# Starting each front one pair earlier, ScalarE on both halves of the features, and the linear attention term once per pair

## The chip, the core and the metric

The kernel runs on one core of a Trainium2 chip. The metric is the time of the device for one execution, in microseconds (us). The engines of the core work side by side, each through its own instructions in the order in which the program put them: TensorE (PE in the profile; PEld is its load of weights) multiplies matrices, VectorE (DVE), ScalarE (ACT) and GpSimd (POOL) work on elements, SyncE (SP) issues transfers. An engine that has to wait for another holds up all that stands behind the waiting instruction.

## The reference

The input x has 64 graphs of 256 nodes with 128 features, in float32, and all share one 256 x 256 matrix adj. Four layers follow each other, each of the form x = x + layer(relu(layernorm(x))). Cut to what matters (e is short for the 256 hidden features of the last layer):

```python
# layer 0: five steps of a gated graph network
m  = adj @ h;  u = h @ u3.T
z, r = sigmoid([m, m] @ w3.T + u), sigmoid([m, m] @ w4.T + u)
hv = tanh([m, m] @ w5.T + (r * h) @ u5.T)
h  = (1 - z) * h + z * hv
# layer 1: h, adj.T h, 2 adj.T adj.T h - h (each twice), one matrix, relu
# layer 2: ((adj + 1) h) @ weight + bias, each row over its norm
# layer 3: attention over all pairs of nodes i, j
pre = s1[:, :, None, :] + s2[:, None, :, :] + b_lin      # 256 x 256 x 256 for each graph
e   = einsum('bije,e->bij', leaky_relu(pre, 0.2), a) + adj
out = sigmoid(softmax(e, axis=2) @ x)
```

Layer 3 is the bulk: for each graph 65536 pairs of nodes with 256 hidden features each, which are clipped and then summed over the features with the weights a. s1 and s2 are x times the two halves of a 256 x 256 matrix W, and in this model W is adj itself.

## The kernel before

**Pairs of graphs.** The 64 graphs are worked on in 32 pairs (`NB = 2`). Most tiles are 128 partitions by 2 x 256 float32, with features on the partitions.

**The front of a pair** (`front`, a Python generator) is all that comes before the attention: layers 0 to 2, the norm of layer 3, its transpose hT, and the operands of the attention. These are s2a (s2 of the first 128 hidden features, with the sign turned; it stays in one of two PSUM banks), s2n (the same for the second 128, copied to SBUF), s1a and s1b (s1 plus b_lin for each half, by ScalarE). It is one long chain: nearly every step needs the one before, on another engine. Three PSUM banks (`spare`) are shared by the fronts in progress and the tails.

**Tiles of the attention.** The leaky relu is split as 0.2 pre + 0.8 relu(pre). For the second part, a "tile" (`rl`, 128 hidden features x 4 nodes i x 2 graphs x 256 nodes j) holds, for four nodes i, either min(s1, -s2) or relu(s2 + s1): both serve, with weights of opposite signs, since they differ by a term that is the same for all j and so drops out of the softmax. A pair has 64 slots for each half of the features, 128 tiles in all:
- VectorE makes every tile of the first half (half 0): one minimum of 2048 elements, line 628, from s1a and the PSUM bank s2a.
- ScalarE and GpSimd share the tiles of the second half (half 1). ScalarE takes eight activations of 256 elements a tile (line 641), from a copy of s2n in PSUM (`s2p`, line 635), GpSimd eight minima of 256 elements (line 647), from s2n in SBUF. An engine makes the next slot of half 1 whenever it is free.
Thirteen buffers `rl` are shared. At most 8, 3 and 2 of them are held by VectorE, ScalarE and GpSimd (`MOST`).

**Scoring.** TensorE multiplies each tile by a window of the weights a (four matmuls of 32 columns each, line 685 in `score`) and sums 64 tiles into one PSUM bank. So a pair has two blocks of 128 nodes i (`ic`), and two banks `pes` take turns. The first thing summed into each block is the linear term 0.2 a W2 h (`project(pe, g2, hT)` in `score`); its part that depends only on i drops out of the softmax.

**The tail of a block** (`tail`): VectorE adds adj to the scores (sc, line 543, which frees the bank), takes the maximum (nmx, line 547), ScalarE the exponential, TensorE transposes and multiplies by h3, ScalarE takes the tanh, GpSimd finishes, SyncE stores.

**What sets the order.** A scheduler in Python, at the end of the kernel, runs while the program is written. It holds a clock for each engine, adds a cost for each group of instructions (`ran`) and, at each step, gives the engine that is furthest behind the most urgent of what is ready by that reckoning: steps of a tail first, then steps of a front, then tiles or scoring. The result is a fixed order of instructions on each engine. `SEEN` is the time until another engine can use a result. Where the order is wrong for the chip, the engines wait for each other's semaphores.

**When fronts run.** Two fronts begin at the start; after that, these lines decide when the next one begins and how fast it may go:

```python
        while begun_fronts[0] < NPAIR and begun_fronts[0] < 2 + scored[0] // (2 * SLOTS):
            begin_front()
...
            due = STEPS_OF_FRONT * (scored[0] / (2 * SLOTS) - (key - 2)) / SPREAD
            if CHAINS[key][2] > due + AHEAD:
                return None
```

A pair has `2 * SLOTS` = 128 tiles, so front p + 2 begins when all tiles of pair p have been scored, which is about when pair p + 1 starts. `due` is how many of a front's 106 steps may have been taken; with `SPREAD` 1.8 and `AHEAD` 8, some 67 of them may be taken at once at that point. A tile of a pair can be made only when its front is done: `READY[p]` holds the operands, and `since` the times at which each half can start.

Of the kernel before, what the change touches and what calls it, by code (L numbers as in the profile page):

```python
# [8 lines left out]
F32 = mybir.dt.float32  # L9
AF = mybir.ActivationFunctionType  # L10
# [5 lines left out]
NB = 2  # L16
# [9 lines left out]
def kernel(  # L26
# [65 lines left out]


    clock = dict.fromkeys((PE, DVE, ACT, POOL), 0.0)
    SEEN = {PE: 0.25, DVE: 0.14, ACT: 0.45, POOL: 0.13}

    def ran(engine, us, *after):
        clock[engine] = max(clock[engine], 0.0, *after) + us
        return clock[engine] + SEEN[engine]

    spare = [[b, 0.0] for b in banks[5:]]

# [34 lines left out]
    def load_x(p):  # L137
        if p >= NPAIR:
            return
        XIN[p] = work.tile([P, NB, NC, D], F32, name="xin", bufs=3)  # L140
        for b in range(NB):
            nc.sync.dma_start(XIN[p][:, b], x[p * NB + b].rearrange("(c p) d -> p c d", p=P))

# [29 lines left out]
    def load_transposed(w, name, scale=None):  # L173

        cols = w.shape[1]
        raw = work.tile([P, 2 * D], F32, name="w_raw", bufs=3)
        nc.scalar.dma_start(raw[:, :cols], w)
        src = raw[:, :D]
        if cols == 2 * D:
            s = work.tile([P, D], F32, name="w_sum")  # L180
            nc.vector.tensor_add(s, raw[:, :D], raw[:, D:])
            src = s
        pt = bank([P, P], "pt")
        nc.tensor.transpose(pt, src, ident)
        t = const.tile([P, P], F32, name=name)
        if scale is None:
            nc.vector.tensor_copy(t, pt)
        else:
            nc.vector.tensor_scalar(t, pt, scale, None, op0=OP.mult)
        return t  # L190
# [44 lines left out]
    nc.vector.memset(win_n, 0.0)  # L235
    w2n = const.tile([P, N], F32, name="w2n")
    nc.vector.tensor_scalar(w2n, adj_t[:, 1, :], -1.0, None, op0=OP.mult)
    a_rep = const.tile([P, NE, P], F32, name="a_rep")
    nc.vector.memset(a_rep, 1.0)
    for k in range(NE):  # L240
        nc.vector.tensor_scalar(win[:, k, 31:32], acol[:, k:k + 1], 1.0 - ALPHA, None, op0=OP.mult)
# [62 lines left out]
    def rows_of(t):  # L304
        return t.rearrange("p b c d -> p (b c) d")

    SHORT = dict(tag="short", bufs=14)


    PROJECT, MIX, TURN, PRODUCT, PRODUCTS = 0.86, 1.74, 0.69, 0.88, 2.64  # L310
# [28 lines left out]
        spare.append([bank[0], t])  # L339
        return c, t  # L340

    KEPT = {"hT": dict(bufs=4), "hT3": {}, "s2n": {}}

    READY = {}

    def front(p):
# [163 lines left out]
        yield PE, max(t_hT, t_s2v[p % 2])  # L510
        project(s2a, w2n[:, 0:P], hT)
        t_s2a = ran(PE, PROJECT, t_hT, t_s2v[p % 2])
        yield PE, t_hT, 1
        b = take()
        project(b[0], w2n[:, P:2 * P], hT)
# [18 lines left out]
        nc.scalar.activation(s1a, by_feature(b[0]), AF.Identity, bias=blin[:, 0:1], scale=1.0)  # L534
        t_n = ran(ACT, BIASED, t)
        spare.append([b[0], t_n])
        READY[p] = dict(x3=x3, h3=h3, hT=hT, s1=(s1a, s1b), s2a=by_feature(s2a), s2n=s2n, since=(max(t_n, t_s2a), max(t_b, t_2)))

    def tail(p, ic, pe, since, x3, h3):

        yield DVE, since
        sc = feat("sc", **SHORT)
        nc.vector.tensor_add(sc, by_feature(pe), adj_n[:, ic, :].unsqueeze(1).to_broadcast([P, NB, N]))
        t_pe[p * NC + ic] = ran(DVE, ELEMENTS, since)
        yield DVE, clock[DVE]
        nmx = work.tile([P, NB], F32, name="nmx")
        nc.vector.tensor_reduce(nmx, sc, AX.X, OP.max, negate=True)
        t = ran(DVE, ELEMENTS)
        yield ACT, t
        sums = work.tile([P, NB], F32, name="sums")  # L550
        for b in range(NB):
            nc.scalar.activation(sc[:, b, :], sc[:, b, :], AF.Exp, bias=nmx[:, b:b + 1], scale=1.0,  # L552
                                 accum_out=sums[:, b:b + 1])
        t_s = ran(ACT, 1.0, t)
        yield PE, t_s, 1
        b = take()
        to_token(b[0], sc)
        t = ran(PE, TURN, t_s, b[1])
        yield ACT, t
        wT = tok("wT", **SHORT)  # L560
        nc.scalar.mul(wT, by_token(b[0]), 0.5)
        t = ran(ACT, COPY, t)
        spare.append([b[0], t])
        yield PE, t, 1
        b = take()
        po = b[0][:, :NB * D].rearrange("p (b d) -> p b d", b=NB)
        for k in range(NB):
            for c in range(NC):
                side_by_side(po[:, k, :], wT[:, k, c, :], h3[:, k, c, :], c == 0, c == NC - 1)
        t = ran(PE, PRODUCT, t, b[1])  # L570
        yield DVE, t_s
        rs = work.tile([P, NB], F32, name="rs")
        nc.vector.reciprocal(rs, sums)
        t_s = ran(DVE, 0.08, t_s)
        yield ACT, max(t, t_s)
        o = work.tile([P, NB, D], F32, name="o")
        for k in range(NB):
            nc.scalar.activation(o[:, k, :], po[:, k, :], AF.Tanh, scale=rs[:, k:k + 1])
        t = ran(ACT, 0.5, t, t_s)
        spare.append([b[0], t])  # L580
        yield POOL, t
        nc.gpsimd.tensor_scalar(o, o, 0.5, 0.5, op0=OP.mult, op1=OP.add)
        nc.gpsimd.tensor_add(o, o, x3[:, :, ic, :])
        ran(POOL, 1.1, t)
        nc.sync.dma_start(out[p * NB:(p + 1) * NB, ic * P:(ic + 1) * P, :].rearrange("b p d -> p b d"), o)
        TAILED.add((p, ic))
# [8 lines left out]
    made = []  # L595
    left = {}
    t_pe = {}
    t_s2v = [0.0, 0.0]
    TAILED = set()

    def where(n):
        return n // SLOTS, n % SLOTS // 32, n % 32

    def tile_ready(e):

        if e in begun:
            return 0.0
        n = following[e != DVE]
        if n >= NSLOT or n // SLOTS not in READY or held[e] == MOST[e] or not tiles:
            return None  # L610
        return max(READY[n // SLOTS]["since"][e != DVE], min(t[1] for t in tiles))

    def work_on_tile(e):
        k = int(e != DVE)
        if e not in begun:
            tiles.sort(key=lambda t: t[1])
            begun[e] = [following[k], *tiles.pop(0), 0]
            following[k] += 1
            held[e] += 1
        n, t, free, part = begun[e]  # L620
        p, ic, r = where(n)
        ops = READY[p]
        i0 = ic * P + r
        since = max(ops["since"][k], free)
        if e == DVE:
            whole = [P, 4, NB, N]
            rows = ops["s1"][0][:, :, i0:i0 + 97:32].rearrange("p b g -> p g b").unsqueeze(3)
            nc.vector.tensor_tensor(t, rows.to_broadcast(whole), ops["s2a"].unsqueeze(1).to_broadcast(whole), op=OP.min)  # L628
            done = ran(DVE, 2.2, since)
            t_s2v[p % 2] = done  # L630
            parts = 1
        elif e == ACT:
            if "s2p" not in ops:
                ops["s2p"] = s2p
                nc.scalar.copy(s2p, ops["s2n"])
                ran(ACT, COPY, since)
            parts = 2
            for g in (2 * part, 2 * part + 1):
                for b in range(NB):
                    i = i0 + g * 32  # L640
                    nc.scalar.activation(t[:, g, b, :], s2p[:, b, :], AF.Relu, bias=ops["s1"][1][:, b, i:i + 1], scale=-1.0)  # L641
            done = ran(ACT, 1.43, since)
        else:
            parts = 4
            for b in range(NB):
                i = i0 + part * 32
                nc.gpsimd.tensor_scalar(t[:, part, b, :], ops["s2n"][:, b, :], ops["s1"][1][:, b, i:i + 1], None, op0=OP.min)  # L647
            done = ran(POOL, 1.8, since)
        begun[e][3] += 1
        if part + 1 == parts:  # L650
            del begun[e]
            made.append((done, n, k, t, e))
# [18 lines left out]
    def score(tile_):  # L671
        since, n, k, t, e = tile_
        p, ic, r = where(n)
        block = p * NC + ic
        pe = pes[block % 2]
        if block not in left:
            left[block] = 64
            project(pe, g2, READY[p]["hT"], stop=False)
            ran(PE, PROJECT, t_pe.get(block - 2, 0.0))
        made.remove(tile_)  # L680
        left[block] -= 1

        w = win if e == ACT else win_n
        for g in range(4):
            nc.tensor.matmul(pe[g * 32:(g + 1) * 32, :], w[:, k, 31 - r:63 - r], flat(t[:, g]),  # L685
                             start=False, stop=(left[block] == 0), skip_group_check=True)
        free = ran(PE, PROJECT, since)
        tiles.append([t, free])
        held[e] -= 1
        scored[0] += 1  # L690
        if left[block] == 0:
            begin((p, ic), tail(p, ic, pe, free, READY[p]["x3"], READY[p]["h3"]))


    CHAINS = {}
    STEPS_OF_FRONT, SPREAD, AHEAD = 106, 1.8, 8
    begun_fronts = [0]

    def begin(key, steps):
# [8 lines left out]
    def chain_ready(key, e):  # L708

        engine, since, bank, gate = (*CHAINS[key][1], 0, None)[:4] if len(CHAINS[key][1]) < 4 else CHAINS[key][1]  # L710
        if engine != e or bank and not spare or gate and not gate():
            return None
        if not isinstance(key, tuple) and key > 0:

            due = STEPS_OF_FRONT * (scored[0] / (2 * SLOTS) - (key - 2)) / SPREAD
            if CHAINS[key][2] > due + AHEAD:
# [12 lines left out]
    for e in clock:  # L729
        clock[e] = 0.0  # L730
    while scored[0] < 2 * NSLOT or CHAINS:
        while begun_fronts[0] < NPAIR and begun_fronts[0] < 2 + scored[0] // (2 * SLOTS):
            begin_front()
        e = min(now, key=now.get)
        todo = []
# [57 lines left out]
```

## Time and profile before

| | before |
|---|---|
| median of 3 runs | 5523.23 us (5520.46 to 5524.22) |
| span of the profiled execution | 5520.6 us |
| mean granted TensorE clock | 0.997 |
| busy: PE, DVE, ACT, POOL | 5376.7, 5314.8, 5012.2, 5038.5 us |
| HBM traffic | 3 GB/s over the span |
| last step of the first front (s1a) | at 145.4 us |
| first pair on DVE | 145.4 to 298.4 us, the second to 469.1 us |
| three pairs in the middle | 1988.6 to 2495.0 us |
| from the start of the last pair to the end | 5364.4 to 5520.6 us |

A group of instructions is read so: line of the kernel, engine, operation, what it writes <- what it reads, shapes, number; then the sum of busy time and the mean of one in ns; then the idle time of the engine just before them, with what ended it. A row of waits reads: who waited <- for whom: us in total, times, longest. A row of windows has the stretch in us from the start, its length, and for each engine busy us with the number of instructions. In the timeline a row has start, length, engine, line, operation and tiles, and in brackets the idle time before it with what ended it. Activations overlap each other, so a mean of one is longer than the spacing. A matmul of the source has two records in the profile.

### The profile page before, as it was taken

What the parts mean: (1) busy time and instruction counts of PE and PEld (TensorE: products, weight loads), DVE (VectorE), ACT (ScalarE), POOL (GpSimd) and SP (SyncE); (2) the same over time, 40 slices, a digit from 0 to 9 for tenths busy, and PEclk for the clock granted to TensorE, in tenths of its full rate; (3) what the DMA queues carried; (4) which work ended last, traced back from release to release, by engine and by line L of the source; (5) the groups of instructions that cost most, each with busy time, mean ns of one, the idle gap of its engine ahead of it and who ended that gap; (6) DMA issues with size and microseconds to landing.
All of it is one profiled execution on the core that took longest, in us unless ns stands there. A gap on an engine that the chain in (4) does not pass through costs nothing.

```text
span 5520.6 us, 138813 instructions
## 1 busy us (share of the span) xinstructions
PE 5376.7 (97%) x56341; PEld 1942.7 (35%) x56341; DVE 5314.8 (96%) x4355; ACT 5012.2 (91%) x13193; POOL 5038.5 (91%) x5854
## 2 busy tenths in 40 slices
PE   6999999999999999999999999999999999999999
PEld 2333333333333333333333333333333333333333
DVE  3999999999999999999999999999999999999999
ACT  3998899989989998999899899989998999999898
POOL 0999999999899999999998999999999989999998
PEclk9999999999999999999999999999999999999999
DMA  0000000000000000000000000000000000000000
GB/s 18 4 5 2 5 6 5 5 3 5 6 5 6 5 3 5 5 5 5 3 5 5 5 5 4 4 6 5 4 5 3 6 5 5 6 4 3 4 4 3
DMA packets 38836, 26.98 MB, mean 5 GB/s; under 512 B 3504, under 2 KB 38192, under 8 KB 38192
## 3 DMA queue, kind: packets, MB, share of 16 engines
q1 hardware_dynamic: 35088, 17.05, 1.0%
q8 instruction: 440, 7.21, 0.6%
q14 instruction: 204, 1.67, 0.1%
q10 hardware_dynamic: 3104, 1.05, 0.1%
HBM read 9.70 MB, written 8.39 MB: 3 GB/s over the span
## 4 chain that ended last, share of the span: by engine, by line
PE 46%; DVE 28%; ACT 22%; issue 3%; POOL 1%; DMA 0%; ACTq 0%; POOLq 0%; SPq 0%; DVEq 0%
PE bank L685 29%; DVE rl L628 22%; ACT rl L641 17%; PE bank L260 15%; PE bank L288 1%; ACT bank L395 1%; DVE stats L320 1%; DVE bank L404 1%; ACT h L331 1%; DVE hT L408 1%; ACT bank L377 1%; DVE d L400 1%; ACT h L419 1%; PE bank L281 1%; ACT sc L552 1%
## 5 line engine op out<-in xcount | busy, mean ns | idle before, releaser
L647 POOL TENSOR_SCALAR rl<-s2n,s1b 128x256 f32<-128x256 f32 x5272 | 4741.5, 937 | 103.5 <-PE bank L685 51.8
L628 DVE TENSOR_TENSOR rl<-s1a,bank 128x2048 f32<-128x2048 f32 x2048 | 4552.1, 2278 | 39.6 <-ACT s1a L534 39.6
L641 ACT ACTIVATE rl<-bank,s1b 128x256 f32<-128x256 f32 x11112 | 4436.2, 978 | 1.0
L685 PE MATMUL bank<-rl,win_n 128*32 128x512 f32 x21656 | 2785.3, 594 | 29.7 <-DVE rl L628 28.4
L685 PE MATMUL bank<-rl,win 128*32 128x512 f32 x11112 | 1598.2, 594 | 0.0
L685 PEld LDWEIGHTS bank<-rl,win_n 128*32 128x32 f32 x21656 | 734.4, 110 | 1487.9 <-issue 1196.7
L685 PEld LDWEIGHTS bank<-rl,win 128*32 128x32 f32 x11112 | 397.0, 110 | 766.7 <-issue 567.0
L260 PE MATMUL bank<-adj_t,h 128*32 128x256 f32 x5120 | 318.1, 382 | 17.0 <-ACT h L419 16.4
L331 ACT ACTIVATE h<-x,mv 128x128 f32<-128x128 f32 x384 | 180.7, 724 | 167.4 <-POOL mv L327 167.4
L254 POOL TENSOR_SCALAR mv<-mv 128x4 f32<-128x4 f32 x128 | 29.6, 231 | 264.7 <-DVE mv L322 260.9
L260 PEld LDWEIGHTS bank<-adj_t,h 128*32 128x32 f32 x5120 | 166.5, 110 | 199.1 <-ACT h L419 89.5
L377 ACT ACTIVATE bank<-bank,gate_b 128x512 f32<-128x512 f32 x160 | 172.7, 1079 | 58.8 <-issue 29.1
L392 ACT ACTIVATE bank<-bank,gate_b 128x512 f32<-128x512 f32 x160 | 176.7, 1105 | 8.9 <-PE bank L260 8.9
L395 ACT ACTIVATE bank<-bank,gate_b 128x512 f32<-128x512 f32 x160 | 170.9, 1068 | 14.3 <-PE bank L260 14.3
L337 ACT COPY mT<-bank 128x512 f32<-128x512 f32 x160 | 165.6, 1035 | 15.7 <-PE bank L260 15.6
L260 PE MATMUL bank<-hT,u3t 128*32 128x512 f32 x1280 | 175.3, 594 | 0.0
L260 PE MATMUL bank<-mT,w4t 128*32 128x512 f32 x1280 | 174.6, 594 | 0.0
L260 PE MATMUL bank<-mT,w 128*32 128x512 f32 x1280 | 174.1, 592 | 0.0
L260 PE MATMUL bank<-rh,u5t 128*32 128x512 f32 x1280 | 174.0, 592 | 0.0
L260 PE MATMUL bank<-mT,w5t 128*32 128x512 f32 x1280 | 174.0, 592 | 0.0
L400 DVE TENSOR_TENSOR d<-bank,hT 128x512 f32<-128x512 f32 x160 | 109.4, 684 | 50.1 <-ACT bank L395 50.1
L419 ACT COPY h<-bank 128x512 f32<-128x512 f32 x128 | 149.1, 1165 | 5.1 <-PE bank L288 5.1
(112 smaller groups left out, 3165.9 us busy)
## 6 DMA issues: line engine op xcount, KB each, us to landing
xin<-in_x_dram SPq DMA_DIRECT2D x64, 128.0 KB, 2.3
out_dram<-o SPq DMA_DIRECT2D x64, 128.0 KB, 1.8
w_raw<-in_L_gnn_w_w_dram ACTq DMA_DIRECT2D x3, 128.0 KB, 2.6
th_raw<-in_L_gnn_Theta_dram ACTq DMA_DIRECT2D x1, 320.0 KB, 3.4
adj_n<-in_adj_dram SPq DMA_DIRECT2D x1, 256.0 KB, 4.7
w_raw<-in_L_gnn_u_w_dram ACTq DMA_DIRECT2D x2, 64.0 KB, 2.3
bias<-in_L_gnn_bias_dram ACTq DMA_DIRECT2D x2, 64.0 KB, 3.3
w<-in_L_gnn_weight_dram ACTq DMA_DIRECT2D x1, 64.0 KB, 3.1
```

The costliest lines, as they stand in the source:

```text
L260: nc.tensor.matmul(o[g:g + 32], w[:, g:g + 32], t, start=start, stop=stop, skip_group_check=True)
L331: nc.scalar.activation(h[:, k, :], s[:, k, :], AF.Relu, bias=mv[:, k, 0:1], scale=mv[:, k, 1:2])
L337: nc.scalar.copy(c, by_feature(bank[0]))
L377: nc.scalar.activation(r[0], pr[0], AF.Tanh, bias=br, scale=0.5)
L392: nc.scalar.activation(pr[0], pr[0], AF.Tanh, bias=bz, scale=0.5)
L395: nc.scalar.activation(pv[0], pv[0], AF.Tanh, bias=bh, scale=1.0)
L400: nc.vector.tensor_sub(d, by_feature(pv[0]), hT)
L419: nc.scalar.copy(h, by_token(b[0]))
L628: nc.vector.tensor_tensor(t, rows.to_broadcast(whole), ops["s2a"].unsqueeze(1).to_broadcast(whole), op=OP.min)
L641: nc.scalar.activation(t[:, g, b, :], s2p[:, b, :], AF.Relu, bias=ops["s1"][1][:, b, i:i + 1], scale=-1.0)
L647: nc.gpsimd.tensor_scalar(t[:, part, b, :], ops["s2n"][:, b, :], ops["s1"][1][:, b, i:i + 1], None, op0=OP.min)
L685: nc.tensor.matmul(pe[g * 32:(g + 1) * 32, :], w[:, k, 31 - r:63 - r], flat(t[:, g]), start=False, stop=(left[block] == 0), skip_group_che ...
```

## The change

It has five parts.

1. **Earlier fronts.** Front p + 2 begins as soon as the first tile of pair p is scored, so two pairs ahead, and is paced from the start: with `AHEAD` 2 and `SPREAD` 1.7 its 109 steps spread over 1.7 pairs. The pace is not applied while no spare bank is free. It is meant to have the operands of a pair ready before the pair starts.
2. **ScalarE helps with half 0** where half 0 has fallen two slots or more behind half 1 (`half`, `LAG`). For that s2 of half 0 is also copied to SBUF in the front (`s2c`).
3. **The linear term once per pair.** It is projected in the front and copied to SBUF (`lin`), and no longer into each block's bank; GpSimd adds it to the scores in the tail, between VectorE's sum with adj and VectorE's maximum.
4. **The scheduler's reckoning of ScalarE.** The lag of its results is 0.18 us instead of 0.45, plus a sum that grows by 2.4% of its busy time and falls in its idle time.
5. **Buffers.** xin has 2 instead of 3, the shared short-lived tiles 12 instead of 14; three tiles of the set-up share these; s2c and lin have two each.

```diff
-    SEEN = {PE: 0.25, DVE: 0.14, ACT: 0.45, POOL: 0.13}
+    SEEN = {PE: 0.25, DVE: 0.14, ACT: 0.18, POOL: 0.13}
+    behind = [0.0]
     def ran(engine, us, *after):
-        clock[engine] = max(clock[engine], 0.0, *after) + us
-        return clock[engine] + SEEN[engine]
+        start = max(clock[engine], 0.0, *after)
+        if engine == ACT:
+            behind[0] = max(0.0, behind[0] - (start - clock[ACT])) + 0.024 * us
+        clock[engine] = start + us
+        return clock[engine] + SEEN[engine] + (behind[0] if engine == ACT else 0.0)
...
-        XIN[p] = work.tile([P, NB, NC, D], F32, name="xin", bufs=3)
+        XIN[p] = work.tile([P, NB, NC, D], F32, name="xin", bufs=2)
...
-    SHORT = dict(tag="short", bufs=14)
+    SHORT = dict(tag="short", bufs=12)
...
+        yield ACT, t_s2a
+        s2c = feat("s2c")
+        nc.scalar.copy(s2c, by_feature(s2a))
+        t_s2c = t_s2a = ran(ACT, COPY, t_s2a)
+        yield PE, t_hT, 1
+        b = take()
+        project(b[0], g2, hT)
+        t = ran(PE, PROJECT, t_hT, b[1])
+        yield ACT, t
+        lin, t_lin = copied("lin", b, t)
...
-        t_pe[p * NC + ic] = ran(DVE, ELEMENTS, since)
-        yield DVE, clock[DVE]
+        t = t_pe[p * NC + ic] = ran(DVE, ELEMENTS, since)
+        ops = READY[p]
+        yield POOL, max(t, ops["t_lin"])
+        nc.gpsimd.tensor_add(sc, sc, ops["lin"])
+        t = ran(POOL, 1.05, t, ops["t_lin"])
+        yield DVE, t
         nmx = work.tile([P, NB], F32, name="nmx")
         nc.vector.tensor_reduce(nmx, sc, AX.X, OP.max, negate=True)
...
+    LAG = 2
+    def half(e):
+        return 0 if e == DVE or e == ACT and following[0] <= following[1] - LAG else 1
...
-                    nc.scalar.activation(t[:, g, b, :], s2p[:, b, :], AF.Relu, bias=ops["s1"][1][:, b, i:i + 1], scale=-1.0)
-            done = ran(ACT, 1.43, since)
+                    nc.scalar.activation(t[:, g, b, :], (s2p if k else ops["s2c"])[:, b, :], AF.Relu,
+                                         bias=ops["s1"][k][:, b, i:i + 1], scale=-1.0)
+            done = ran(ACT, 1.43 if k else 1.6, since)
...
-        if block not in left:
+        first = block not in left
+        if first:
             left[block] = 64
-            project(pe, g2, READY[p]["hT"], stop=False)
-            ran(PE, PROJECT, t_pe.get(block - 2, 0.0))
...
-                             start=False, stop=(left[block] == 0), skip_group_check=True)
-        free = ran(PE, PROJECT, since)
+                             start=first, stop=(left[block] == 0), skip_group_check=True)
+        free = ran(PE, PROJECT, since, t_pe.get(block - 2, 0.0))
...
-    STEPS_OF_FRONT, SPREAD, AHEAD = 106, 1.8, 8
+    STEPS_OF_FRONT, SPREAD, AHEAD = 109, 1.7, 2
...
-        if not isinstance(key, tuple) and key > 0:
+        if not isinstance(key, tuple) and key > 0 and spare:
...
-        while begun_fronts[0] < NPAIR and begun_fronts[0] < 2 + scored[0] // (2 * SLOTS):
+        while begun_fronts[0] < NPAIR and begun_fronts[0] < 2 + (scored[0] + 2 * SLOTS - 1) // (2 * SLOTS):
```

More of the change, by code (lines that the diff above doesn't have):

```diff
@@ L175, in load_transposed @@
         cols = w.shape[1]
-        raw = work.tile([P, 2 * D], F32, name="w_raw", bufs=3)
+        raw = work.tile([P, 2 * D], F32, name="w_raw", tag="short", bufs=12)
         nc.scalar.dma_start(raw[:, :cols], w)
@@ L179, in load_transposed @@
         if cols == 2 * D:
-            s = work.tile([P, D], F32, name="w_sum")
+            s = work.tile([P, D], F32, name="w_sum", tag="short", bufs=12)
             nc.vector.tensor_add(s, raw[:, :D], raw[:, D:])
@@ L237 @@
     nc.vector.tensor_scalar(w2n, adj_t[:, 1, :], -1.0, None, op0=OP.mult)
-    a_rep = const.tile([P, NE, P], F32, name="a_rep")
+    a_rep = work.tile([P, NE, P], F32, name="a_rep", tag="short", bufs=12)
     nc.vector.memset(a_rep, 1.0)
@@ L340, in copied @@
         return c, t
-    KEPT = {"hT": dict(bufs=4), "hT3": {}, "s2n": {}}
+    KEPT = {"hT": dict(bufs=4), "hT3": {}, "s2n": {}, "lin": {}}
     READY = {}
@@ L536, in front @@
         spare.append([b[0], t_n])
-        READY[p] = dict(x3=x3, h3=h3, hT=hT, s1=(s1a, s1b), s2a=by_feature(s2a), s2n=s2n, since=(max(t_n, t_s2a), max(t_b, t_2)))
+        READY[p] = dict(x3=x3, h3=h3, hT=hT, s1=(s1a, s1b), s2a=by_feature(s2a), s2c=s2c, s2n=s2n, lin=lin, t_lin=t_lin,
+                        since=(max(t_n, t_s2a, t_s2c), max(t_b, t_2)))
     def tail(p, ic, pe, since, x3, h3):
@@ L543, in tail @@
         nc.vector.tensor_add(sc, by_feature(pe), adj_n[:, ic, :].unsqueeze(1).to_broadcast([P, NB, N]))
-        t_pe[p * NC + ic] = ran(DVE, ELEMENTS, since)
-        yield DVE, clock[DVE]
+        t = t_pe[p * NC + ic] = ran(DVE, ELEMENTS, since)
[4 more added lines that the diff above has]
+        yield DVE, t
         nmx = work.tile([P, NB], F32, name="nmx")
         nc.vector.tensor_reduce(nmx, sc, AX.X, OP.max, negate=True)
-        t = ran(DVE, ELEMENTS)
+        t = ran(DVE, ELEMENTS, t)
         yield ACT, t
@@ L607, in tile_ready @@
             return 0.0
-        n = following[e != DVE]
+        n = following[half(e)]
         if n >= NSLOT or n // SLOTS not in READY or held[e] == MOST[e] or not tiles:
             return None
-        return max(READY[n // SLOTS]["since"][e != DVE], min(t[1] for t in tiles))
+        return max(READY[n // SLOTS]["since"][half(e)], min(t[1] for t in tiles))
     def work_on_tile(e):
-        k = int(e != DVE)
         if e not in begun:
+            k = half(e)
             tiles.sort(key=lambda t: t[1])
-            begun[e] = [following[k], *tiles.pop(0), 0]
+            begun[e] = [following[k], k, *tiles.pop(0), 0]
             following[k] += 1
             held[e] += 1
-        n, t, free, part = begun[e]
+        n, k, t, free, part = begun[e]
         p, ic, r = where(n)
@@ L632, in work_on_tile @@
         elif e == ACT:
-            if "s2p" not in ops:
+            if k and "s2p" not in ops:
                 ops["s2p"] = s2p
@@ L648, in work_on_tile @@
             done = ran(POOL, 1.8, since)
-        begun[e][3] += 1
+        begun[e][4] += 1
         if part + 1 == parts:
```

## The prediction

> **What bounds the kernel now.** I read the page first (shares of busy time, then the costly groups), then busy time by windows, then the waits, and last the timeline of single engines where the windows dip.
>
> ```profile
> PE 5376.7 (97%) x56341; PEld 1942.7 (35%) x56341; DVE 5314.8 (96%) x4355; ACT 5012.2 (91%) x13193; POOL 5038.5 (91%) x5854
> L647 POOL TENSOR_SCALAR rl<-s2n,s1b 128x256 f32<-128x256 f32 x5272 | 4741.5, 937 | 103.5 <-PE bank L685 51.8
> L628 DVE TENSOR_TENSOR rl<-s1a,bank 128x2048 f32<-128x2048 f32 x2048 | 4552.1, 2278 | 39.6 <-ACT s1a L534 39.6
> L641 ACT ACTIVATE rl<-bank,s1b 128x256 f32<-128x256 f32 x11112 | 4436.2, 978 | 1.0
> ```
>
> Every engine is over 90% busy, so the page alone doesn't say which one binds. It does say who makes what: DVE makes all 2048 tiles of the first half of the features, ACT (11112/8 = 1389) and POOL (5272/8 = 659) the 2048 tiles of the second. The next view is busy time in a stretch that begins and ends at the same point of the cycle.
>
> ```profile
> core 0: us, PE busy (x) PEld busy (x) DVE busy (x) ACT busy (x) POOL busy (x), PEclk, DMA share, GB/s
> 1988.60:2495.00 506.40, 498.57 (x5280) 179.26 (x5280) 497.24 (x406) 468.67 (x1236) 473.77 (x551) 1.00 0.02 5
> 1968.00:1988.00 20.00, 19.17 (x176) 5.43 (x168) 19.90 (x32) 12.40 (x32) 10.11 (x15) 1.00 0.00 1
> 2141.00:2161.00 20.00, 18.07 (x148) 5.35 (x144) 14.66 (x30) 8.39 (x22) 11.65 (x18) 1.00 0.01 2
> ```
> ```profile
> L647 POOL TENSOR_SCALAR rl<-s2n,s1b 128x256 f32<-128x256 f32 x496 | 446.1, 935 | 9.2 <-PE bank L685 4.8 <-ACT s1b L525 4.3
> L628 DVE TENSOR_TENSOR rl<-s1a,bank 128x2048 f32<-128x2048 f32 x192 | 427.0, 2278 | 2.9 <-ACT s1a L534 2.9
> L641 ACT ACTIVATE rl<-bank,s1b 128x256 f32<-128x256 f32 x1040 | 416.4, 936 | 0.1
> ```
>
> The second fence is the groups of the same 506.4 us: 192 tiles of DVE are three pairs, so a pair takes 168.8 us. In it DVE is busy 497.24/3 = 165.7 us (98.2%), ACT 156.2, POOL 157.9. DVE binds. PE's 98.5% is not load alone[...]. I price PE by runs without gaps in the chain of waits and the timeline: 16 L685 records (two tiles) in 1.72 us, so 0.86 a tile; a whole mix of nodes 1.73; four transposes 0.66; eight records of 128 columns follow each other by 0.22. A pair: 128 x 0.86 + 31 projections x 0.86 + 8 mixes x 1.73 + 10 transposes x 0.66 + 24 small groups x 0.22 = 110.1 + 26.7 + 13.8 + 6.6 + 5.3 = 162.5 us. So PE has 6 us a pair free, DVE 3.
>
> The two 20 us rows lie just before a new pair starts. ACT and POOL fall to 8 to 12 us of 20, in the second DVE too. The reason is in the timeline of POOL:
>
> ```profile
> 1970.74 5.43 POOL L647 TENSOR_SCALAR rl<-s2n,s1b 128x256 f32<-128x256 f32 x6
> 1977.16 0.23 POOL L254 TENSOR_SCALAR mv<-mv 128x4 f32<-128x4 f32 x1 [0.98 <-DVE mv L322]
> ...
> 1987.28 0.23 POOL L254 TENSOR_SCALAR mv<-mv 128x4 f32<-128x4 f32 x1 [8.49 <-DVE mv L322]
> ...
> 1988.89 6.33 POOL L647 TENSOR_SCALAR rl<-s2n,s1b 128x256 f32<-128x256 f32 x7
> ```
>
> Between 1976 and 1989 POOL has no tile: the old pair's are all taken, and the next pair's s1b, written at 1986.28 by the last steps of its front, is not there. A front starts only when the second pair before its own is wholly scored (the stats of a new xin stand at 465.4, 633.1, 809.5 us, its s1a at 641.6, 804.8, 975.5), so it takes 166 to 176 us, as long as a pair. It is ready just in time or late, and DVE waits for it:
>
> ```profile
> DVE d L400 <- ACT bank L395: 50.1, 31, 5.1
> DVE rl L628 <- ACT s1a L534: 39.6, 21, 10.3
> DVE rs L573 <- ACT sc L552: 29.9, 11, 2.9
> ```
>
> **What the Trainium skill says.** "Perfetto Trace Analysis", Identifying the Most-Contended Engine, takes occupancy as fair for Vector, Scalar and GPSIMD and not for matmuls; this trace agrees, PE showing 98.5% over a load of 162.5/168.8 = 96%. "VectorE: DVE Perf Modes", The perf-mode tier table, gives an fp32 tensor_tensor of 2048 elements 2293 ns, with no faster mode; L628 takes 2278, so a tile can't become cheaper on DVE and can only go elsewhere. "GPSIMD Engine Reference", 3.1, has about 2.6 cycles an element for the two-input add; at the 1.2 GHz of its reconciliation, 512 elements are an estimated 1.1 us. The trace has L583, 256 elements, at 738 ns, and a 4-element add (L327) at 201, so 0.2 + 2 x 0.54 = 1.28. I take 1.2, ends 1.05 and 1.5.
>
> **The change part by part.** Counts are from the order of the built program, which has no times.
>
> 1. *ScalarE takes tiles of the first half.* Tiles on DVE go from 2048 to 2015; ACT makes 33 (264 activations) from s2c and s1a, about one a pair. DVE: 33 x 427.0/192 = 33 x 2.224 = 73.4 us less. This lies on the engine that binds.
> 2. *What ACT and POOL give for it.* ACT makes 1382 tiles of the second half instead of 1389, so 26 more in all: 26 x 8 x 416.4/1040 = 26 x 3.20 = 83 us. The helper reads SBUF and not PSUM; "Perfetto Trace Analysis", Optimizing Scalar/DVE Operations, has 93 against 51 ns of fixed cost, so an estimated 8 x 42 ns a tile, 11 us. POOL does 5328 instead of 5272 minima: 56 x 446.1/496 = 50 us.
> 3. *Two copies a pair on ACT*, s2c and lin: the like copies of s2n stand at 0.58 (L337, L635), so 64 x 0.59 = 38 us.
> 4. *The linear term once a pair.* PE does one projection by g2 instead of two: 32 x 0.86 = 27.5 us less. Not on DVE's path, but PE is the second in load.
> 5. *The sum on POOL in the tail*: 64 x 1.2 = 77 us of POOL. It is also a new wait: the maximum L547, which followed its sum at once, now follows POOL's. POOL may be inside two minima (1.8 us) when the sum is ready. In the new order DVE has one more tile (2.2 us) between the two in most of the 64 tails and none in the others; behind the waiting maximum stand DVE's tiles and the front's elements. Bounds: nothing, and 64 x 1.0 = 64 us; I take 16. The score bank is freed by the first sum, as before, so PE doesn't see it.
> 6. *Fronts begin one pair earlier and are paced over 1.7 pairs.* No work moves between engines. The operands of a pair are ready well before it starts: the 39.6 us of DVE for s1a go, and so do the stretches in which ACT and POOL have no tile. This is the part that makes room for items 2, 3 and 5.
> 7. *The scheduler's new lag of ACT, fewer buffers (xin 2, short 12), s2c and lin.* Durations don't change. Two fronts overlap for 0.7 of a pair with three spare banks; a front now has 281 us instead of 168, so I count this at nothing, with waits of up to 1 us a pair as the upper end. DMA moves 5 GB/s and hides.
>
> Load of a pair: DVE 165.7 - 73.4/32 = 163.4; PE 162.5 - 0.86 = 161.6; ACT 156.2 + (83 + 11 + 38)/32 = 160.3; POOL 157.9 + (50 + 77)/32 = 161.9. DVE still binds, by 1.5 us.
>
> The sum, on DVE: the first s1a was ready at 145.4 us, and 2 us more for three steps added to the front: 147. DVE was busy 45.4 us until then, so 5314.8 - 45.4 = 5269.4 after; less 73.4 is 5196. Its idle time after 145.4 was 5375.2 - 5269.4 = 105.8 (5375.2 is 5520.6 - 145.4), of which about 11 are the last tail and 95 lie between. Of the 95, 40 go (item 6) and 16 come (item 5): 71. So 147 + 5196 + 71 + 11 = 5425, and 3 more, as the median before stands 2.6 over the profiled span: **5428 us**, 1.7% less.
>
> **The rivals.**
>
> *B, more than that:* waits such as d on L395 (50.1 us) also come from ACT being late through the rush of the front, and a paced front loses them: 30 us of idle time left, 5387. For it: those waits lie in the front's steps. Against: all engines get fuller.
>
> *C, gain eaten by balance:* four engines within 3.1 us of each other, in a fixed order, wait for each other in turn. If PE keeps all of today's gap between load and period (168.8 - 162.5 = 6.3 us), a pair takes 161.6 + 6.3 = 167.9; forecast A has 163.4 + 71/31 = 165.7. Between them, at 167, 30 pairs x 1.8 = 54 us go: 5470. POOL's sums at 1.5 us would push the same way. For it: PE waits for tiles, hT and h today. Against: those waits are shorter where DVE is less late.
>
> *D, slower:* if the idle time of POOL (168.8 - 157.9 = 10.9 a pair) is the fixed cost of waiting inside norm and tail, and not want of tiles, then 161.9 + 10.9 = 172.8 a pair, 30 x 4 = 120 us more: 5643. For it: its waits are named norm (14.3 of some 29 us in the three pairs) and tail (5.5). Against: the timeline shows those waits where no tile was to be had.
>
> *E, no change:* the wait for the maximum and for buffers eats just what item 1 gives, 5520.
>
> **How the numbers follow.** A (5428) 0.54, B 0.17, C 0.17, E 0.03, D 0.09. Faster: A, B and C, 0.88. The range reaches from 5378, a little under B, to 5492, above C, and leaves out D, E and tails of the others.
>
> **What would show it.** DVE at 163 to 164 us busy a pair, 165 to 166 of period; the wait of L628 for s1a gone; no dip of ACT and POOL before a pair; the new sum at 1.05 to 1.5 us; ACT and POOL at 96% or more. It would be wrong if a wait of DVE's maximum for POOL runs to over 60 us, if DVE falls under 97% in a steady pair while PE or POOL stands at 98%, or if the dips stay.

## The result, and the profile after

The changed kernel takes 5354.04 us (5352.97 to 5354.87, 4 runs) against 5522.57 for the kernel before: a ratio of 0.9695, with a 95% interval from 0.9678 to 0.9712. That is 3.05% less, where 1.7% was forecast, and below the lower end of the range, 5378.

The page of the changed kernel has these lines for those shown of before (lines of the kernel have moved: 628 is now 652, 641 is 665, 647 is 672, 547 is 566, 685 is 709):

```profile
PE 5241.4 (98%) x56085; PEld 1861.5 (35%) x56085; DVE 5221.7 (98%) x4322; ACT 5121.4 (96%) x13465; POOL 5160.9 (96%) x5974
L672 POOL TENSOR_SCALAR rl<-s2n,s1b 128x256 f32<-128x256 f32 x5328 | 4786.0, 940 | 9.7 <-ACT s1b L539 9.7
L652 DVE TENSOR_TENSOR rl<-s1a,bank 128x2048 f32<-128x2048 f32 x2015 | 4484.6, 2276 | 12.1 <-ACT s1a L548 12.1
L665 ACT ACTIVATE rl<-bank,s1b 128x256 f32<-128x256 f32 x11056 | 4392.2, 839 | 1.3
```

All engines are busy for a larger share of the time, and DVE makes 33 tiles less. POOL's idle time before its tiles fell from 103.5 us to 9.7, DVE's wait for s1a from 39.6 to 12.1, and that in a single wait, for the first pair. Busy time by windows of the changed kernel follows: first up to the first tile of DVE, then the steady part, the last 87 us, and the 20 us before ACT turns to a new pair. A row has start and length, the busy us of PE, PEld, DVE, ACT and POOL, then the granted clock, the DMA share and GB/s:

```profile
0.00:140.90 140.90, 100.15 (x1057) 40.50 (x1057) 45.00 (x128) 47.00 (x82) 9.86 (x24) 0.89 0.06 16
468.80:4959.70 4490.90, 4460.46 (x48172) 1592.94 (x48168) 4473.74 (x3691) 4373.63 (x11513) 4447.32 (x5146) 1.00 0.02 5
5265.70:5352.40 86.70, 69.55 (x620) 20.14 (x611) 71.22 (x38) 74.27 (x205) 74.81 (x85) 0.95 0.01 4
...
2077.60:2097.60 20.00, 20.00 (x204) 6.69 (x200) 19.96 (x13) 19.80 (x53) 20.00 (x23) 1.00 0.01 2
```

In the steady part DVE is busy 4473.74 of 4490.90 us, 99.6%; before it was 98.1% (4641.73 of 4731.00). The dip of ACT and POOL before a new pair is gone: 19.80 and 20.00 of 20 us, where they had 12.40 and 10.11. A pair takes 163.5 us instead of 168.8, as the starts of sc in the second and the 29th pair tell (398.6 and 4814.2 us over 27 pairs; before, 394.3 and 4951.4).

What DVE waits for in the steady part, first the kernel before (469.1 to 5200.1 us), then the changed one (468.8 to 4959.7):

```profile
DVE rs L573 <- ACT sc L552: 28.8, 10, 2.9
DVE rl L628 <- ACT s1a L534: 26.5, 19, 2.8
DVE d L400 <- ACT bank L395: 8.0, 18, 0.5
DVE rh L381 <- ACT bank L377: 6.0, 19, 0.5
```
```profile
DVE nmx L566 <- POOL sc L562: 8.1, 16, 1.0
DVE x L499 <- POOL rn L259: 0.4, 1, 0.4
DVE rn L490 <- ACT sq L486: 0.3, 1, 0.3
DVE rh L385 <- ACT bank L381: 0.2, 1, 0.2
```

Not only the wait for the front's operands (s1a) went, but the waits for ACT inside the fronts (d, rh) and tails (rs) with it. What is left is mostly the new wait that the change itself brought, of the maximum nmx for POOL's sum, at 8 us.

So DVE's time is made up like this, from the windows of both kernels:

| us | before | forecast | after |
|---|---|---|---|
| until the first tile | 145.4 | 147 | 140.9 |
| DVE busy after that | 5269.4 | 5196 | 5176.7 |
| DVE idle between, up to the end piece | 95 | 71 | 19.3 |
| DVE idle in the end piece | 11 | 11 | 15.5 |
| sum | 5520.6 | 5425 | 5352.4 |

The end piece is the last 156 us before and the last 87 us after; over 156 us the changed kernel would have 16.3 there and 18.5 between. Of the 73 us that the forecast of 5425 was too high, 52 are idle time, 19 busy time and 6 the start; the end takes 4 back.

### The profile page after: what moved, and what is told of

The parts are those of the page before. It is cut to its first block, busy times and chain, and to the rows that moved or that the text cites. A ratio compares the mean times of both kernels' runs of the same rounds, so it can differ in the third digit from the quotient of the medians.

```text
span 5352.4 us, 138977 instructions
## 1 busy us (share of the span) xinstructions
PE 5241.4 (98%) x56085; PEld 1861.5 (35%) x56085; DVE 5221.7 (98%) x4322; ACT 5121.4 (96%) x13465; POOL 5160.9 (96%) x5974
## 3 DMA queue, kind: packets, MB, share of 16 engines
q10 hardware_dynamic: 3104, 1.05, 0.1%
## 4 chain that ended last, share of the span: by engine, by line
PE 49%; DVE 34%; POOL 9%; ACT 5%; issue 4%; DMA 0%; POOLq 0%; SPq 0%; DVEq 0%; ACTq 0%
PE bank L709 32%; DVE rl L652 28%; PE bank L264 15%; POOL rl L672 7%; ACT rl L665 3%; PE bank L292 1%; DVE d L404 1%; DVE stats L324 1%; DVE bank L408 1%; DVE hT L412 1%; DVE rh L385 1%; PE bank L285 1%; POOL sc L562 0%; DVE mv L327 0%; POOL mv L259 0%
## 5 line engine op out<-in xcount | busy, mean ns | idle before, releaser
L652 DVE TENSOR_TENSOR rl<-s1a,bank 128x2048 f32<-128x2048 f32 x2015 | 4484.6, 2276 | 12.1 <-ACT s1a L548 12.1
L665 ACT ACTIVATE rl<-bank,s1b 128x256 f32<-128x256 f32 x11056 | 4392.2, 839 | 1.3
L709 PE MATMUL bank<-rl,win_n 128*32 128x512 f32 x21448 | 2654.8, 593 | 33.9 <-DVE rl L652 31.9
L709 PE MATMUL bank<-rl,win 128*32 128x512 f32 x11320 | 1487.2, 593 | 0.0
L709 PEld LDWEIGHTS bank<-rl,win_n 128*32 128x32 f32 x21448 | 678.9, 110 | 1496.4 <-issue 1214.0
L709 PEld LDWEIGHTS bank<-rl,win 128*32 128x32 f32 x11320 | 365.9, 110 | 754.4 <-issue 630.2
L341 ACT COPY mT<-bank 128x512 f32<-128x512 f32 x160 | 133.9, 837 | 33.1 <-PE bank L264 24.6
L396 ACT ACTIVATE bank<-bank,gate_b 128x512 f32<-128x512 f32 x160 | 141.0, 881 | 17.7 <-PE bank L264 17.7
L381 ACT ACTIVATE bank<-bank,gate_b 128x512 f32<-128x512 f32 x160 | 140.0, 875 | 15.6 <-PE bank L264 15.2
L399 ACT ACTIVATE bank<-bank,gate_b 128x512 f32<-128x512 f32 x160 | 136.3, 852 | 12.8 <-PE bank L264 12.8
L423 ACT COPY h<-bank 128x512 f32<-128x512 f32 x128 | 117.3, 916 | 29.6 <-PE bank L292 24.7
L404 DVE TENSOR_TENSOR d<-bank,hT 128x512 f32<-128x512 f32 x160 | 108.4, 678 | 37.5 <-ACT bank L399 37.5
```

What stands on the lines that cost most here:

```text
L341: nc.scalar.copy(c, by_feature(bank[0]))
L381: nc.scalar.activation(r[0], pr[0], AF.Tanh, bias=br, scale=0.5)
L396: nc.scalar.activation(pr[0], pr[0], AF.Tanh, bias=bz, scale=0.5)
L399: nc.scalar.activation(pv[0], pv[0], AF.Tanh, bias=bh, scale=1.0)
L404: nc.vector.tensor_sub(d, by_feature(pv[0]), hT)
L423: nc.scalar.copy(h, by_token(b[0]))
```

## The experiments

The parts of the change were taken out one at a time, put alone into the kernel before, and in two runs varied. The theory was that early fronts give the engines tiles at all times and take DVE's waits away, and that the help takes work off DVE. The rivals tried were that the new reckoning of ScalarE removed the waits, that the moved linear term did by relieving PE, and that the help alone is what pays.

**The old reckoning.**

```diff
-    SEEN = {PE: 0.25, DVE: 0.14, ACT: 0.18, POOL: 0.13}
+    SEEN = {PE: 0.25, DVE: 0.14, ACT: 0.45, POOL: 0.13}
...
-            behind[0] = max(0.0, behind[0] - (start - clock[ACT])) + 0.024 * us
+            behind[0] = max(0.0, behind[0] - (start - clock[ACT])) + 0.0 * us
```

> The changed kernel with the scheduler's old reckoning of ScalarE (lag 0.45 us, nothing that grows). The order has 2013 tiles on DVE instead of 2015. Theory 1 (want of tiles: once fronts are early, the engines always have tiles, and DVE's idle time goes whatever the reckoning): within 10 us of 5354. Theory 2 (the new reckoning is what took DVE's idle time from some 95 us to about 20 between the first tile and the last tail, beyond the 40 us of the wait for s1a): about 5400, with waits of DVE for ACT (rs, d, rh) of 40 us or more in the steady pairs.

Measured: 5356.72 us (5345.36 to 5357.31). Theory 2 falls: with early fronts the reckoning makes no difference that can be seen, and from 470 to 4950 us DVE waits for ACT for 0.2 us in all. Three of the four times lie at 5357 and one at 5345, for one and the same program, so a difference of some 10 us between two programs has to be read with care.

**No help from ScalarE on the first half.**

```diff
-        return 0 if e == DVE or e == ACT and following[0] <= following[1] - LAG else 1
+        return 0 if e == DVE else 1
```

> The changed kernel in which ScalarE makes no tile of the first half; s2c is still copied. DVE makes 2048 tiles, 33 more. If DVE binds with next to no idle time, 33 x 2.22 = 73 us come back: 5427. If other engines (PE, POOL) set the pace of the changed kernel, part of it hides: under 5400. If the help matters more than its own work (balance between the halves), over 5440.

Measured: 5415.50 us, 61 more than the changed kernel, between the 5427 and the 5400 of the first two cases. The help is worth most of its 73 us of work, as it is if DVE binds, and the other 106 us of the gain on the kernel before (5520.98 beside this run) come without it.

**The linear term back on PE** (the projection by g2 at the head of each block, no lin, no sum on POOL):

```diff
-        nc.gpsimd.tensor_add(sc, sc, ops["lin"])
...
             left[block] = 64
+            project(pe, g2, READY[p]["hT"], stop=False)
+            ran(PE, PROJECT, t_pe.get(block - 2, 0.0))
...
```

> The changed kernel with the linear term projected into each block's bank again, no lin and no sum on POOL. The order has 2025 tiles on DVE, 10 more, as POOL is free for 7 more tiles and ACT takes fewer. If DVE binds: 10 x 2.22 = 22 us more, less the 8 us that the maximum waits for POOL: 5368. If PE is what binds: 32 x 0.86 = 27 us more than 5354, 5381 or over. If POOL's sum and the longer tail cost more than they bring: under 5354.

Measured: 5354.59 us, no difference. None of the three values came: 27.5 us of PE (an estimate, at 0.86 us a projection) and 84 us of POOL were exchanged and nothing followed. PE is not what binds, and the order finds another balance: ACT helps with 23 tiles where it had 33, and the 13 us more that DVE is busy are made up by 13 us less of idle time, 10 of which are the maximum's waits for POOL.

**Early fronts alone, in the kernel before.**

```diff
-    STEPS_OF_FRONT, SPREAD, AHEAD = 106, 1.8, 8
+    STEPS_OF_FRONT, SPREAD, AHEAD = 106, 1.7, 2
...
-        if not isinstance(key, tuple) and key > 0:
+        if not isinstance(key, tuple) and key > 0 and spare:
...
-        while begun_fronts[0] < NPAIR and begun_fronts[0] < 2 + scored[0] // (2 * SLOTS):
+        while begun_fronts[0] < NPAIR and begun_fronts[0] < 2 + (scored[0] + 2 * SLOTS - 1) // (2 * SLOTS):
```

> The kernel before with only its fronts early and paced (begin at the first scored tile of the second pair before, 1.7 and 2, pace only while a bank is spare). Old reckoning, linear term on PE, no help, old buffers; 2048 tiles on DVE. Theory 1 (early fronts alone remove the waits): as the changed kernel without help, 5410 to 5425, DVE over 99% busy in the middle. Rival (it takes the new reckoning or the moved linear term too): 5440 to 5500.

Measured: 5406.74 us (5406.44 to 5406.97), a ratio of 0.9791 (0.9775 to 0.9807). These few lines give 115.6 us, over two thirds of the whole, and the time is 3 us under the range of theory 1, far from that of the rival. Of the three waits that the prediction shows for the kernel before, this is left (the 40.0 us of d and the 11.7 us of s1a lie ahead of the first tile):

```profile
DVE d L400 <- ACT bank L395: 40.0, 10, 5.1
DVE rl L628 <- ACT s1a L534: 11.7, 1, 11.7
DVE rs L573 <- ACT sc L552: 1.2, 1, 1.2
```

The windows of this run, to be read as above:

```profile
0.00:146.50 146.50, 100.94 (x1057) 41.55 (x1057) 44.87 (x127) 45.84 (x80) 10.04 (x24) 0.86 0.07 17
146.50:5405.20 5258.70, 5179.27 (x55288) 1830.95 (x55284) 5238.05 (x4228) 4944.67 (x13082) 5041.88 (x5863) 1.00 0.02 5
```

DVE makes the same 2048 tiles as before. After the first tile it is idle 20.7 us instead of 105.8, tail included, and it is busy 5238.1 us instead of 5269.4, though its instructions are the same. The last section says where the busy time went. The first tile is at 146.5 us here. It comes at 139 to 144 us in all ten kernels with the new buffers, and at 146 to 147 in the three without, of which the next has only the 12 short tiles. So the earlier start goes with the buffers; whether it is xin or the shared tiles of the set-up was not tried.

**The help alone, in the kernel before** (s2c, `half` and the choice of operands as in the change, 12 short tiles for room):

> The kernel before with only the help of ScalarE on the first half (and s2c; 12 short tiles for room). The order has 1984 tiles on DVE, 64 helped. If DVE's work sets the time of the kernel before: 64 x 2.22 = 142 us less, about 5380. If the late front sets it (a pair can't be shorter than its front), the gain is lost as waiting: 5480 to 5530, with longer waits for s1a.

Measured: 5493.83 us (5485.56 to 5494.11), ratio 0.9945 (0.9930 to 0.9960). DVE makes 64 tiles less, 142 us of work, and the kernel gains 28. The rest came back as waiting. In the profile, which is of the fastest of the four times, DVE is idle for 209 us after the first tile, where it was 106, most of it in three waits that come in nearly every pair:

```profile
DVE rl L638 <- ACT s1a L538: 77.4, 29, 11.7
DVE sc L547 <- PE bank L695: 60.5, 29, 4.5
DVE rs L577 <- ACT sc L556: 42.9, 29, 3.0
```

So while fronts are late, work taken off the busiest engine is of little use. s1a comes every 167.7 us here, pair after pair, and a front takes 176 us from its first statistics to s1a. That the late front is what sets the pair is read from these waits and from the runs with early fronts, in which the same kind of help pays in full (below).

**Late fronts, all else as changed**, with the new reckoning, with the old one, and with the short lag but without the part that grows:

```diff
-    STEPS_OF_FRONT, SPREAD, AHEAD = 109, 1.7, 2
+    STEPS_OF_FRONT, SPREAD, AHEAD = 109, 1.8, 8
...
-        while begun_fronts[0] < NPAIR and begun_fronts[0] < 2 + (scored[0] + 2 * SLOTS - 1) // (2 * SLOTS):
+        while begun_fronts[0] < NPAIR and begun_fronts[0] < 2 + scored[0] // (2 * SLOTS):
```

> The changed kernel with fronts that begin as before (second pair before scored in full; 1.8 and 8), all else as changed. The order has 2000 tiles on DVE, 48 helped, so DVE has 33 us less work than in the changed kernel. Theory 1 (early fronts are what pays): pairs of 167 to 169 us, 5470 to 5510, with the dips of ACT and POOL before a pair back. Rival (the help and the reckoning pay, early fronts little): 5350 to 5390.

> The changed kernel with late fronts, as the run of 6080 us, but with the old reckoning of ScalarE. Theory (the growing lag is added to every ScalarE step of a front in the reckoning, so a front on the critical path is planned too slowly; 0.024 of 150 us is 3.6 us a step): the loss of 560 us goes, 5450 to 5550. If lateness with help or the tail on POOL is the cause: still near 6080.

> Late fronts as in the runs of 6080 and 5536 us, with the short lag of 0.18 us for ScalarE but without the part that grows with its busy time. If the growing part is what made the late fronts so slow: 5480 to 5580. If the short lag is (results expected too early, engines waiting in turn): 5800 or over.

Measured: 6080.43, 5536.53 and 5483.98 us. The first was a miss of 570 us: the operands of one pair came 102 to 106 us after those of the last, those of the next 263 to 280 us later, in turn, and between two pairs there was a stretch without tiles: DVE made none for 83 us, from 1561 on. That stretch, and the next, from the first of the three runs:

```profile
1530.00:1650.00 120.00, 101.94 (x1131) 38.59 (x1126) 66.93 (x97) 70.40 (x162) 50.33 (x63) 0.97 0.02 5
1650.00:1750.00 100.00, 94.43 (x984) 33.11 (x977) 99.86 (x80) 100.00 (x275) 99.02 (x117) 1.00 0.02 5
```

DVE is busy for 66.93 of 120 us in the first, 99.86 of 100 in the second. The last run tells the cause apart: the growing part of the lag does it, since without it the kernel with late fronts takes 5484 us. That it acts by delaying each ScalarE step of a front in the reckoning was argued beforehand and is not shown by itself. With early fronts the same reckoning does no harm (the first experiment), most likely because nothing waits for the front there. With the old reckoning on both sides, late fronts take 5536.53 us and early ones 5356.72 (the first experiment), so within the changed kernel the early fronts alone are worth 180 us.

**Early fronts without a pace** (`AHEAD` 1000 in the changed kernel):

> The changed kernel with early fronts that are not paced. If being early is what pays: within 15 us of 5354. If the pace matters (a rush of front steps keeps DVE, ACT and PE waiting for each other, as in the kernel before): 5380 or over. The order has only 9 helped tiles, 24 fewer, which alone is 24 x 2.22 = 53 us on DVE: 5407 if DVE binds.

Measured: 5420.57 us (two times, 5420.38 and 5420.76), 67 more than the changed kernel. 53 of these are the 24 tiles that ACT didn't take off DVE, so the rush costs the balance more than it causes waits. After the first tile DVE has no wait of d or rh for ACT and 1.2 us of rs, so it is the early start, and not the pace, that took these away.

**Early fronts and the help, without the two other parts** (the edits of the first and the third experiment together):

> Early, paced fronts and the help of ScalarE, with the new buffers, but the linear term on PE and the old reckoning of ScalarE. If these two parts are the whole gain: 5345 to 5362, the same as the changed kernel. If the moved linear term and the new reckoning each stand in for the other: over 5370.

Measured: 5355.53 us (5355.23 to 5357.29). Early fronts and the help, with the buffers, are the whole gain. The help, 24 tiles here or 53 us of work, is worth 51 us on top of early fronts (5406.74), where 142 us of it were worth 28 with late ones.

**The measured cost of POOL's sum told to the scheduler.**

```diff
-        t = ran(POOL, 1.05, t, ops["t_lin"])
+        t = ran(POOL, 1.32, t, ops["t_lin"])
```

> The changed kernel, with the scheduler told 1.32 us for POOL's sum instead of 1.05, as it was measured. DVE makes 2016 tiles, one more. If the waits of the maximum for POOL (10.3 us) come from this error: they go, 5345. If they come from something else, or other waits take their place: within 5 us of 5354.

Measured: 5337.41 us (5336.21 to 5338.07), ratio 0.9668 (0.9653 to 0.9682), the fastest of all. The sum had been reckoned at 1.05 us and takes 1.3. The waits of the maximum for it, of the changed kernel and then of this one:

```profile
DVE nmx L566 <- POOL sc L562: 10.3, 18, 1.4
```
```profile
DVE nmx L566 <- POOL sc L562: 2.3, 4, 1.4
```

Eight of the 17 us are these waits. Some 7 more are DVE's busy time, 5215.1 us against 5221.7 with one more tile. Reckoned from start to start, so that no waiting is hidden in busy time, the delays just before the maximum fell by about 12 us and those before DVE's tiles by about 7; why the latter fell was not tried. Each kernel's four times lie within 2 us, so the 17 us are real, but they belong to one order and need not follow from the same correction in another.

## Why the prediction was wrong

The direction, the engine that binds and the cause were right. The size was not, and one step carries most of it: "Of the 95, 40 go (item 6) and 16 come (item 5): 71." What went was 76 on balance, and 19.3 is left. Early fronts were credited only with the 39.6 us that the profile names as waiting for s1a, and 10.3 of these are the wait for the first pair, which is over when the first tile begins. It is no part of the 95, fronts that start earlier can't take it since the first one starts at once, and it stands at 12.1 us in the changed kernel. The run with early fronts alone shows what they are worth: 85 us of DVE's idle time and 31 us of its busy time. Of the 85, some 29 are waits for s1a, 29 those of rs for ACT, 16 those of d and rh, and the rest shorter gaps. All went with the same few lines, so they had the same cause and bore other names.

Point by point:

- *Item 1, the help on DVE:* right. 33 tiles of 2.276 us are 75 us, and the durations of all DVE instructions fell by 75 (5621.6 to 5546.5). In time it is worth 61.
- *Item 2, ACT's and POOL's share:* right. A helped activation starts 399 ns after the one before, against 357 for one from PSUM, so 42 ns more, just what the estimate took from the Trainium skill's 93 and 51 ns ("Perfetto Trace Analysis", Optimizing Scalar/DVE Operations).
- *Item 4, PE relieved:* right that it lies on no path; the run without it is the same.
- *Item 5, POOL's sum:* 84.3/64 = 1.32 us, between the ends of 1.05 and 1.5 and over the 1.2 taken. Its wait was 10.3 us for the 16 forecast.
- *Item 6, early fronts:* the cause was named rightly and priced at a third: 40 of the 115.6 us that they give alone.
- *Item 7, reckoning and buffers:* priced at nothing. The reckoning is nothing here. With the buffers goes a start about 5 us earlier, where the forecast had put it 2 us later. A front takes 272 us, about the 281 that were reckoned.
- *DVE's busy time:* 5196 forecast, 5176.7 measured. The error was to take busy time as work: 18 of the 19 us are more overlap between instructions, as the last section explains.
- *The load of a pair:* DVE 163.4 forecast and 4473.74/4490.90 x 163.5 = 162.9 measured; ACT 160.3 and 159.2; POOL 161.9 and 161.9. The period followed DVE's load within 0.6 us, where the forecast had left 2.3 for waits.

Of the rivals, B was nearest: more waits go than those for s1a, but at 5387 it was still 33 us high. Its example, d with 50.1 us, was misread, since 40.0 of these lie ahead of the first tile, where 37.5 stayed; and the rush that it gave as the reason is not borne out, since the waits stay away without a pace too. C, four full engines that hold each other up, did not happen: in the steady part they were busy 99.3, 99.6, 97.4 and 99.0% of the time at once. D fell with the dips: POOL waited 131.7 us for the norm's mv and 50.2 for the tail's o in the steady part before, and 0.9 and nothing after. E, no change, fell with the measured time.

## What to carry to other kernels

Where the busiest engine stands at 98% and the others dip at one point of every cycle, look first at what becomes ready there. Here it was a chain as long as the cycle, and work taken off the busiest engine came back as waiting (142 us off, 28 gained) until the chain started earlier. When a cause of waiting is removed, count all waits that go back to it and not only those that bear its name, and leave out those that lie where it can't act. In an order that is planned ahead, put measured durations into the plan: here one cost corrected from 1.05 to 1.32 us came with 17 us.

## What the runs showed of the hardware

Busy time on DVE is not work alone. Most instructions of DVE start before the record of the one in front has ended, by 0.08 us in the median, and the overlap counts once. One that has to wait loses this overlap. In the kernel before, 674 of 4355 DVE instructions started without overlap, and overlap came to 306.8 us of 5621.6 us of durations; with early fronts alone, 325 of 4355, and 334.2 of 5617.1. So of the 31.9 us by which busy time fell with the same instructions, 27 are overlap won back: delay that had stood in the profile as busy time. Between the same two kernels PE, too, has the same 56341 records, and is busy for 5280.2 us instead of 5376.7.

ACT's durations tell even less of work. The activations of a tile start every 357 ns, before as after, and yet in an unbroken row each record is about 8 ns longer than the one in front. They go from 449 to 2896 ns in the kernel before, and fall back, often to some 475 ns, when ACT has been idle for over half a microsecond. By the profile the result is that late: of 111 weight loads of PE in that kernel that were released by an activation whose record is over 1500 ns long, none started before its end, and 91 started within 60 ns after it. The means are 978 ns before (L641), 839 after (L665) and 1694 in the run of 6080 us, at one and the same spacing. So they tell when ACT's results can be used, and not what an activation costs ACT. Why the records grow is not shown.
